# Seven-for-eight products taken one level further in v and p, with another test of the score bound and narrower reciprocals, in an attention and non-local kernel

## The chip, the cores and the metric

The kernel runs on one core of a Trainium2 chip, as one program. The metric is its device time in microseconds: the median of several runs. A core has TensorE (PE, with the weight loads shown apart as PEld), VectorE (DVE), ScalarE (ACT), GpSimd (POOL) and SyncE (SP, which here only issues DMAs). PE writes to PSUM alone: eight banks, each of 512 float32 numbers on 128 partitions. DVE and ACT read results out of there.

## What is computed

Two layers on x of shape (8, 512, 32, 32), all in float32. Layer 0 is attention with 8 heads over the 1024 positions of an image, layer 1 a non-local block with a normalization over the batch. Cut to what matters:

```python
q = conv1x1(x, Wq, bq); k = conv1x1(x, Wk, bk); v = conv1x1(x, Wv, bv)    # B, 8 heads, 64, 1024
attn = softmax(einsum('bhdn,bhdm->bhnm', q, k) * 64 ** -0.5, axis=-1)
x = x + conv1x1(einsum('bhnm,bhdm->bhdn', attn, v), Wp, bp)
g, theta, phi = conv1x1(x, g_w, g_b), conv1x1(x, theta_w, theta_b), conv1x1(x, phi_w, phi_b)
f = einsum('bcn,bdn->bcd', theta, phi) / 1024
z = conv1x1(einsum('bcd,bdn->bcn', f, g), W_w, W_b) + x
out = (z - mean(z)) * rsqrt(var(z) + 1e-5) * gamma + beta                   # over batch and positions
```

## The kernel before

**Stages.** The eight images go one after the other, and their stages are interleaved. In one turn b of the main loop: attention of image b; then q of image b+1, v of b+1, k of b+1; then the projection p of image b, theta and phi (tp), g with f in its midst (pg, pf), the product of f with W (pwf) and z. The last turns differ somewhat, and the last stage of all adds up z of the last images, takes the statistics and writes the outputs.

**Seven products.** A matrix product is cut into quadrants 11, 12, 21, 22, and seven products of sums of quadrants stand for the eight plain ones (the Winograd form of Strassen's method). `seven` (line 258) issues them. Sums of data quadrants, called t1 to t4, are DVE instructions into blocks of 128 x 1024 in a ring of ten (`ring`, tag e), which attention's exponentials use too. Sums of weights are made once and kept in DRAM (`keep`, `keep_inner`), from where each stage's weights are loaded again, two stages ahead.

**Products within products.** For q and k (and, for images 1 to 6, p) some of the seven are themselves replaced by seven smaller ones, the inner steps (`nested`, line 242). `INNER` says which: products 1, 2 and 6 for q and k, 1 and 2 for p, none for v. The inner steps need inner differences of their data quadrant, four DVE instructions of 128 x 256 each (`inner_sums`, `inner_parts`). Where three are replaced, the four left are issued in halves (`HALVES`), 16 units of PE work, and `STEPS` says how many inner steps follow each unit: none after units 0 to 2, one after 3 and 4, two after 5 to 12, one after 13 to 15. `READS` says after which units the finished quadrants are read out of PSUM. Where two are replaced there are 20 units and one step after each from unit 4 on.

**Banks.** PSUM is used as four pairs of banks (`bank`, tags s0 to s3). The inner steps have two pairs. The seven steps of an inner product go to three accumulators, in the order A B A B A C A, and each step's sum is read out by DVE (or ACT, where it is the first of its quadrant) before the accumulator is added to again. For every second inner product the two pairs change places, and its columns are the other half of each bank.

**Order.** The program is compiled by a scheduler that may move instructions, but those passed through `pe`, `dve` and `sp` stay in program order on their engine. All matmuls are. `fills` calls functions after given units of a stage, `between` after given products; in this way DVE work is placed by hand.

**The denominators.** Attention sums its exponentials over keys in `acc`; DMAs fold them into a tile `fold` with few partitions per head. `all_denominators` (line 526) lets PE add up the rest (`den`), takes the reciprocal on DVE as 128 x 512, where eight partitions hold the same row, writes 16 rows to DRAM, and `rows_of` reads them back, each row spread over 64 partitions, into `r`. `normalize` gives four DVE products of o by r, pinned. All of it lies in v of the next image: denominators after its product 1, the products after its product 5. t1 to t4 of o follow in k (line 901), and p needs them.

**The bound.** Exponentials are taken without subtracting the maximum. `bound_scores` (line 421) guards that: DVE takes the largest absolute value of q and k per channel (`peak_of`, line 396), PE adds their products per head (`heads`), DVE compares with `BOUND`, and POOL multiplies q by the outcome, 0 or 1. At the end the outcomes are counted, and if one is 0, a second, slower program (`shifted`) does the work anew.

Of the kernel before, what the change touches and what calls it, by code (L numbers as in the profile page):

```python
# [8 lines left out]
F32 = mybir.dt.float32  # L9
# [7 lines left out]
P = 128  # L17
HEADS = 8
EPS = 1e-5
BOUND = 60.0  # L20
# [10 lines left out]
def unshifted(ctx: ExitStack, tc: tile.TileContext, a: dict, out: bass.AP):  # L31
# [83 lines left out]
    INNER = {"WqT": (1, 2, 6), "WkT": (1, 2, 6), "WpT": (1, 2)}  # L115
# [26 lines left out]
    def weights(name, sums_done=False):  # L142

        n, w = loaded.pop(0)
        assert n == name
        if name not in kept:
            if not sums_done:
                weight_sums(w, corner[name])
            if name not in ("WqT", "WkT"):
                keep("plain" if name == "WpT" else name, w)  # L150
        return w
# [93 lines left out]
    def nested(name, stage, w, data, tags, first, add):  # L245

        slots = [bank(tag, f"{name}_in_{tag}") for tag in tags]
        goes_to = {1: ("11", "21", False), 6: ("12", "22", False), 2: ("21", "t4", True)}
        for n, (q, di, begins) in enumerate(goes_to[i] for i in INNER[stage]):
            a, d = inner_blocks(w, stage, n), data[f"inner {di}"]  # L250
            pair = slots[::-1] if n % 2 else slots
            begun = set()
            for _, wi, di, s, reads in SEVEN:
                ps = pair[s % 2 if s < 2 else 1][:, s // 2, n % 2 * 256:(n % 2 + 1) * 256]
                pe(nc.tensor.matmul(ps, a[wi], d[di], start=s not in begun, stop=True, skip_group_check=True))  # L255
                begun.add(s)
                for to, is_first in reads:
                    c = rows(q).start + int(to[0]) - 1
                    at = cols(q).start + (int(to[1]) - 1) * 256
                    (first if is_first and begins else add)((slice(c, c + 1), slice(at, at + 256)), ps)  # L260
                yield

    def seven(name, w, data, positions_out, first, add, between=None, early=False,
# [10 lines left out]
        if inner:  # L274
            free[:] = [tags[1], tags[2], tags[3], tags[0]]
            steps = nested(name, inner, w, data, tags[2:], first, add)
# [6 lines left out]
        for n, m in HALVES if three else ((n, None) for n in range(len(products))):  # L283
# [12 lines left out]
            work = [(*part, k) for part in (parts if m is None else parts[m:m + 1]) for k in range(nk)]  # L296
            if by_chunk and what in ("11", "s1t1"):
                work.sort(key=lambda one: one[4])
            for to_ps, at, lhsT, rhs, k in work:
                pe(nc.tensor.matmul(to_ps, lhsT(k), rhs(k), start=(s, at) not in begun, stop=(k == nk - 1),  # L300
                                    skip_group_check=True))
                begun.add((s, at))
                for ahead in (True, False):
                    for one, to, is_first in READS.get(unit, ()) if three and ahead == (unit < 15) else ():
                        read(((to, is_first),), slots[one])
                    for _ in range(next(counts, 0) if ahead else 0):
                        next(steps)
                if unit in fills:
                    fills[unit]()
                unit += 1  # L310
# [18 lines left out]
    heads = const.tile([P, P], F32, tag="heads", name="heads")  # L329
    nc.vector.memset(heads, 0.0)  # L330
# [13 lines left out]
    for i in range(WARM):  # L344
        pe(nc.tensor.matmul(ps[:, :P], heads, heads, start=True, stop=True))
# [18 lines left out]
    for j in range(2):  # L364
        nc.vector.memset(heads[j * D:(j + 1) * D, j * D:(j + 1) * D], 1.0)
    mv = const.tile([P, CC, 2], F32, tag="mv", name="mv")
    gates = const.tile([P, B * NPAIR], F32, tag="gates", name="gates")
# [9 lines left out]
    def heads_of(b, what, w, bias, data, pin=lambda ins: None, later=None, **how):  # L377

        t = mats.tile([P, CC, N], F32, tag=what, name=f"{what}_{b}")
        peak = small.tile([P, CC], F32, tag=f"peak_{what}", name=f"peak_{what}_{b}")  # L380

        def first(q, ps):
            if isinstance(q[0], slice):
                c = q[0].start
                nc.scalar.activation(t[:, c, q[1]], ps, AF.Identity, bias=bias[:, c:c + 1])
                return
            for m in range(2):
                c = rows(q).start + m
                if how.get("early") and q == "21":
                    nc.vector.tensor_scalar(t[:, c, cols(q)], ps[:, m, :], bias[:, c:c + 1], 1.0, ALU.add, ALU.mult)  # L390
                else:
                    nc.scalar.activation(t[:, c, cols(q)], ps[:, m, :], AF.Identity, bias=bias[:, c:c + 1])

        seven(f"p{what}_{b}", w, data, False, first, add_to(t, pin), **how)

        def peak_of(c):
            ins = nc.vector.tensor_reduce(peak[:, c:c + 1], t[:, c, :], AX.X, ALU.max, apply_absolute_value=True)
            if b == 0 or later is not None:
                dve(ins)

        for c in range(CC):
            if later is None:
                peak_of(c)
            else:
                later.append(lambda c=c: peak_of(c))
        return t, peak

    def values(b, w, data, between=None):
        v = mats.tile([P, NB, C], F32, tag="v", name=f"v_{b}")

        def at(q):
            return v[:, (int(q[1]) - 1) * NB // 2:int(q[1]) * NB // 2, (int(q[0]) - 1) * C // 2:int(q[0]) * C // 2]

        def as_v(ps):
            return ps.rearrange("p h (i f) -> p (h i) f", f=C // 2)

        seven(f"pv_{b}", w, data, True, lambda q, ps: nc.scalar.copy(at(q), as_v(ps)),  # L417
              lambda q, ps: dve(nc.vector.tensor_tensor(at(q), at(q), as_v(ps), ALU.add)), between)
        return v

    def bound_scores(b, q, k, peak_q, peak_k):

        nc.vector.tensor_tensor(peak_q, peak_q, peak_k, ALU.mult)
        ps = next_bank(f"bound_{b}")[:, 0, :]
        pe(nc.tensor.matmul(ps[:, :CC], heads, peak_q, start=True, stop=True))
        gate = gates[:, b * NPAIR:(b + 1) * NPAIR]
        nc.vector.tensor_scalar(gate, ps[:, :CC], BOUND / SCALE, 1.0, ALU.is_le, ALU.mult)  # L427
        for p in range(NPAIR):
            nc.gpsimd.tensor_scalar(q[:, p, :], q[:, p, :], gate[:, p:p + 1], 1.0, ALU.mult, ALU.mult)  # L429
# [6 lines left out]
    def attention(b, q, k, v, near_end, make_f=None):  # L436
# [89 lines left out]
        def all_denominators(ps):  # L526

            t = folded.pop("t")
            if b == 0:
                bias_product(t[:, 3, :], ps[:, 1, :CC])  # L530
            t, ps = t[:, 2, :], ps[:, 0, :]
            columns(ps, folds8, lambda j: t[:, j * 512:(j + 1) * 512])
            ri = t[:, :512]
            nc.vector.reciprocal(ri, ps)
            d = dram2.tile([16, 512], F32, tag="den", name=f"den_d_{b}")
            nc.sync.dma_start(d, ri.rearrange("(a s) n -> a s n", a=16)[:, 0, :])
            d = d.rearrange("(j g i) n -> g j (i n)", j=2, g=2)
            return d[0], d[1]

        def denominators(g, ps):  # L540
# [8 lines left out]
            d = dram2.tile([8, 512], F32, tag=f"den{g}", name=f"den_d_{b}_{g}")  # L549
            nc.sync.dma_start(d, ri.rearrange("(a s) n -> a s n", a=8)[:, 0, :])  # L550
            return d.rearrange("(j i) n -> j (i n)", j=2)
# [23 lines left out]
        for i in range(len(steps) + LAG):  # L575
# [8 lines left out]
            if b == 0 and i == 8:  # L584
                aside = join_bias(folded["t"][:, 3, :])
# [167 lines left out]
    late, z = {}, {}  # L753
# [90 lines left out]
    q, peak_q = heads_of(0, "q", weights("WqT", True), bq, data, early=True, by_chunk=True)  # L844
# [8 lines left out]
    k, peak_k = heads_of(0, "k", w, bk, data)  # L853
    keep_inner("WkT", w)
    load_w(nc.sync)
    v = values(0, weights("WvT"), data, {3: lambda: bound_scores(0, q, k, peak_q, peak_k)})
    load_w(nc.sync)
    held = {}
    for b in range(B):
# [23 lines left out]
        if not last:  # L883
            later, of_22, of_t4 = [], [], []
# [5 lines left out]
            q, peak_q = heads_of(b + 1, "q", weights("WqT"), bq, nxt["data"], dve, inner="WqT",  # L890
                                 later=later, fills=fills)
            load_w(nc.sync)

            def norm():
                nxt["products"] = normalize(denominators(next_bank(f"den_{b}")))

            v = values(b + 1, weights("WvT"), nxt["data"], {1: norm, 2: lambda: [one() for one in later], 5: lambda: nxt["products"]()})
# [7 lines left out]
            else:  # L905
                w_p = loaded[1][1]
                for unit, which in ((12, (3, 4)), (14, (5, 6))):
                    fills[unit] = lambda which=which: weight_sums(w_p, corner["WpT"], which, dve)
            later_k = []
            k, peak_k = heads_of(b + 1, "k", weights("WkT"), bk, nxt["data"], later=later_k, inner="WkT",  # L910
                                 fills=fills)
            if b:
                inner_sums(nxt["o"], "t4", dve)
            load_w(nc.sync)
# [22 lines left out]
        elif b > B - LATE and b != B - 2:  # L937
# [3 lines left out]
                       {5: lambda: b < B - 2 and of_theta.append(f_sums(b, tps[0], 0)), 1: lambda: [one() for one in later_k[:2]], 2: lambda: [one() for one in later_k[2:]],  # L941
                        4: lambda: bound_scores(b + 1, q, k, peak_q, peak_k)})
# [20 lines left out]

    last_z()


    good = const.tile([P, 1], F32, tag="good", name="good")
    nc.vector.tensor_reduce(good, gates, AX.X, ALU.min)
# [215 lines left out]
```

## Time and profile before

| | us |
|---|---|
| median of 3 runs | 2146.78 (2145.57 to 2147.17) |
| span of the profiled execution | 2143.6 |
| one turn of the loop, images 1 to 4 (606.52 to 869.50 in the chain of waits) | 262.98 |
| of it attention (606.46 to 716.48) | 110.0 |
| q, v, k, p, tp of image 2 | 22.91, 25.38, 22.80, 23.21, 24.40 |

In the profile, a line of groups gives busy time and the mean length of one instruction; matmuls overlap, so their pace is read from the starts of a row of them rather than from that mean. Each float32 matmul leaves two records. "idle before" is how long the engine stood before an instruction, and who released it. A stage's name is that of its PSUM tile: pq, pv, pk, pp, ptp, pg, pf, pwf, pz; those of inner steps end in in_s.

### The profile page before, as it was taken

To read this page: it belongs to the slowest core of one execution; us is meant where nothing else is said; L and a number is where in the kernel's file an instruction comes from. 1 tells how busy PE (TensorE), PEld (TensorE's weight loads), DVE (VectorE), ACT (ScalarE), POOL (GpSimd) and SP (SyncE) were. 2 spreads that over 40 slices of the span, in tenths; PEclk is the share of its full clock that TensorE was granted. 3 is DMA by queue.
4 is the path that set the end of the run, shared out by engine and by line. 5 is a ranking of instruction groups with operands and counts; after the bars stand their busy time and mean duration, and the time that the engine had idled before them with its cause. 6 is when DMAs were issued, how large, how long until landed. Compare 5 with 4: busy or idle time off the path is not lost.

```text
span 2143.6 us, 30444 instructions
## 1 busy us (share of the span) xinstructions
PE 2119.6 (99%) x12654; PEld 1123.3 (52%) x12654; DVE 1448.4 (68%) x1795; ACT 742.8 (35%) x848; POOL 193.2 (9%) x242
## 2 busy tenths in 40 slices
PE   9999999999999999999999999999999999999996
PEld 4534664356733567335673366633666347743462
DVE  6467667667676676766667667676675676756736
ACT  1464104641046310463105621066212652056106
POOL 0111000110001100011001100011000110011000
PEclk9999999999999999999999999999999999999998
DMA  6433443334143331433323342233434235122758
GB/s 242 137 46 58 136 166 127 49 71 129 73 131 49 79 116 73 133 50 83 109 102 109 48 100 99 97 107 50 108 132 161 42 45 139 52 60 39 227 197 341
DMA packets 53969, 231.05 MB, mean 108 GB/s; under 512 B 9792, under 2 KB 16192, under 8 KB 46272
## 3 DMA queue, kind: packets, MB, share of 16 engines
q1 hardware_dynamic: 42144, 199.26, 27.5%
q0 software_dynamic: 10192, 28.46, 11.0%
q8 instruction: 101, 1.65, 0.3%
q10 hardware_dynamic: 1488, 1.32, 0.2%
q14 instruction: 44, 0.36, 0.1%
HBM read 141.84 MB, written 46.27 MB: 88 GB/s over the span
## 4 chain that ended last, share of the span: by engine, by line
PE 96%; ACT 1%; DVE 1%; DMA 1%; issue 0%; SPq 0%; ACTq 0%; DVEq 0%
PE ps L462 21%; PE po L488 21%; PE pv L300 9%; PE ptp L300 9%; PE pp L300 7%; PE pk L300 6%; PE pq L300 5%; PE pg L300 4%; PE pk_in_s L255 3%; PE pq_in_s L255 3%; PE pz L300 2%; PE pf L658 2%; PE pp_in_s L255 2%; PE pwf L713 1%; ACT z L830 1%; PE pf L674 1%
## 5 line engine op out<-in xcount | busy, mean ns | idle before, releaser
L465 ACT ACTIVATE e<-ps 128x1024 f32<-128x1024 f32 x512 | 522.6, 1024 | 431.1 <-PE ps L462 425.6
L471 DVE TENSOR_TENSOR acc<-acc,e 128x1024 f32<-128x1024 f32 x384 | 470.0, 1224 | 143.7 <-ACT e L465 140.3
L462 PE MATMUL ps<-q,k 64*64 64x512 f32 x4096 | 529.4, 589 | 0.0
L488 PE MATMUL po<-e,v 64*64 64x512 f32 x4096 | 528.7, 589 | 0.0
L488 PEld LDWEIGHTS po<-e,v 64*64 64x64 f32 x4096 | 156.6, 133 | 282.9 <-issue 275.4
L462 PEld LDWEIGHTS ps<-q,k 64*64 64x64 f32 x4096 | 155.5, 133 | 283.8 <-issue 274.8
L501 POOL DMA_DIRECT2D fold<-acc x189 | 147.1, 779 | 978.9 <-DMA fold<-acc 576.6
L701 ACT ACTIVATE g<-pg,gb 128x512 f32<-128x512 f32 x31 | 21.3, 687 | 475.4 <-PE pg L300 475.3
L469 DVE TENSOR_TENSOR acc<-e,e 128x1024 f32<-128x1024 f32 x64 | 78.3, 1224 | 136.6 <-ACT e L465 136.6
L300 PE MATMUL pv<-w_WvT,t_x 128*128 128x256 f32 x512 | 116.4, 381 | 0.0
L300 PE MATMUL ptp<-w_tp,t_x 128*128 128x256 f32 x512 | 114.4, 379 | 0.0
L417 ACT COPY v<-pv 128x1024 f32<-128x1024 f32 x32 | 32.4, 1012 | 213.9 <-PE pv L300 213.9
L300 PEld LDWEIGHTS pv<-w_WvT,t_x 128*128 128x128 f32 x512 | 96.6, 190 | 18.5 <-issue 5.7
L300 PEld LDWEIGHTS ptp<-w_tp,t_x 128*128 128x128 f32 x512 | 97.3, 190 | 13.2
L300 PE MATMUL pq<-t_x,w_WqT 128*128 128x512 f32 x200 | 100.1, 592 | 0.8 <-DVE t_x L842 0.8
L300 PE MATMUL pp<-t_o,w_WpT 128*128 128x512 f32 x208 | 100.8, 592 | 0.0
L300 PE MATMUL pk<-t_x,w_WkT 128*128 128x512 f32 x200 | 100.0, 592 | 0.0
L429 POOL TENSOR_SCALAR q<-q,gates 128x1024 f32<-128x1024 f32 x32 | 35.1, 1109 | 718.4 <-DVE gates L427 718.4
L300 PE MATMUL ptp<-w_tp,x 128*128 128x256 f32 x384 | 87.4, 381 | 0.0
L300 PE MATMUL pv<-w_WvT,x 128*128 128x256 f32 x384 | 86.8, 379 | 0.0
L324 DVE TENSOR_TENSOR q<-q,pq_in_s 128x256 f32<-128x256 f32 x119 | 48.6, 420 | 51.1 <-PE pq_in_s L255 38.4
L324 DVE TENSOR_TENSOR k<-k,pk_in_s 128x256 f32<-128x256 f32 x119 | 47.9, 420 | 48.6 <-PE pk_in_s L255 36.0
(195 smaller groups left out, 2348.6 us busy)
## 6 DMA issues: line engine op xcount, KB each, us to landing
fold<-acc POOLq DMA_DIRECT2D x189, 128.0 KB, 3.1
w_WqT<-kept_WqT SPq DMA_DIRECT2D x7, 2368.0 KB, 8.8
w_WkT<-kept_WkT SPq DMA_DIRECT2D x7, 2368.0 KB, 8.8
r<-den_d SPq DMA_DIRECT2D x32, 512.0 KB, 6.9
x<-in_x_dram SPq DMA_DIRECT2D x30, 512.0 KB, 5.7
w_WpT<-kept_WpT SPq DMA_DIRECT2D x6, 2176.0 KB, 8.3
w_WvT<-kept_WvT SPq DMA_DIRECT2D x7, 1792.0 KB, 7.2
w_tp<-kept_tp SPq DMA_DIRECT2D x7, 1792.0 KB, 7.3
```

The lines of the kernel that those rows point to most:

```text
L255: pe(nc.tensor.matmul(ps, a[wi], d[di], start=s not in begun, stop=True, skip_group_check=True))
L300: pe(nc.tensor.matmul(to_ps, lhsT(k), rhs(k), start=(s, at) not in begun, stop=(k == nk - 1), skip_group_check=True))
L324: pin(nc.vector.tensor_tensor(at, at, ps if len(ps.shape) == 3 else ps.unsqueeze(1), ALU.add))
L417: seven(f"pv_{b}", w, data, True, lambda q, ps: nc.scalar.copy(at(q), as_v(ps)), lambda q, ps: dve(nc.vector.tensor_tensor(at(q), at(q), a ...
L429: nc.gpsimd.tensor_scalar(q[:, p, :], q[:, p, :], gate[:, p:p + 1], 1.0, ALU.mult, ALU.mult)
L462: pe(nc.tensor.matmul(ps[c * P // 2:(c + 1) * P // 2, j, :], k[r, p, keys], q[r, p, h * 512:(h + 1) * 512], start=True, stop=True, skip_gr ...
L465: nc.scalar.activation(e, ps, AF.Exp, scale=SCALE)
L469: nc.vector.tensor_tensor(accs[u], es[u, 0], e, ALU.add)
L471: ins = nc.vector.tensor_tensor(accs[u], accs[u], e, ALU.add)
L488: pe(nc.tensor.matmul(ps[j * D:(j + 1) * D, r, :], v[keys, m, (2 * p + j) * D:(2 * p + j + 1) * D], e[keys, j, :], start=(m == 0), stop=(m ...
L501: nc.gpsimd.dma_start(to, part_of, accum_op=ALU.add)
L658: pe(nc.tensor.matmul(to, theta[l][:, i, :], phi[r][:, i, :], start=(i == 0), stop=(i == NB // 2 - 1), skip_group_check=True))
```

## The change

There are four parts.

- v gets inner products: `INNER` has v with products 1, 2 and 6. In v, positions are on the partitions of the result, so an inner step is two matmuls with 128 columns each, and the two pairs of banks do not change places, which leaves one bank free. Into that bank the denominators are summed. The 32 matmuls of the four products left are taken two to a unit. The kept WvT holds its inner sums.
- p gets a third inner product, 6, which needs the inner differences of quadrant 22 of o; they are made after k, behind those of t4. p is now issued in halves, with `STEPS` and `READS` of three.
- The bound is tested on the denominators. `heads`, `peak_of`, `bound_scores`, the gates and POOL's products are gone. All denominators are kept in `dens` (128 x 512), and at the end DVE tests that each lies between 1e-20 and 1e20.
- The reciprocals are taken on 128 x 64: ACT copies the sums out of PSUM, a DMA writes 16 rows to DRAM, a DMA reads them back as 128 rows of 64, DVE takes the reciprocal into `dens`, a DMA writes that to DRAM, and from there r is read as before. Sums are issued after unit 3 of v, the reciprocal and r after unit 8, the products of o by r after unit 15, the last one.

The sums of k and its reads are now pinned with `dve`. The last image's denominators, whose reciprocal stays 128 x 512, are read into `dens` by two DMAs ahead of the last stage. The small product for the bias of p (image 0 alone), which was taken beside its denominators, stands ahead of v.

```diff
-BOUND = 60.0
+SANE = 1e20
...
-    INNER = {"WqT": (1, 2, 6), "WkT": (1, 2, 6), "WpT": (1, 2)}
+    INNER = {"WqT": (1, 2, 6), "WkT": (1, 2, 6), "WvT": (1, 2, 6), "WpT": (1, 2, 6)}
...
-    def nested(name, stage, w, data, tags, first, add):
+    def nested(name, stage, w, data, tags, first, add, positions_out=False):
         slots = [bank(tag, f"{name}_in_{tag}") for tag in tags]
+        if positions_out:
+            rest["bank"] = slots[0][:, 1, :]
...
-            pair = slots[::-1] if n % 2 else slots
+            pair = slots[::-1] if n % 2 and not positions_out else slots
...
-                pe(nc.tensor.matmul(ps, a[wi], d[di], start=s not in begun, stop=True, skip_group_check=True))
+                if positions_out:
+                    ps = ps.rearrange("p (i f) -> p i f", f=P)
+                    for i in range(2):
+                        pe(nc.tensor.matmul(ps[:, i, :], d[di][:, i * P:(i + 1) * P], a[wi], start=s not in begun and not i,
+                                            stop=True, skip_group_check=True))
+                else:
+                    pe(nc.tensor.matmul(ps, a[wi], d[di], start=s not in begun, stop=True, skip_group_check=True))
...
-            work = [(*part, k) for part in (parts if m is None else parts[m:m + 1]) for k in range(nk)]
+            each = len(parts) // 2
+            work = [(*part, k) for part in (parts if m is None else parts[m * each:(m + 1) * each]) for k in range(nk)]
...
+                if three and positions_out and not i % 2:
+                    continue
...
-    def bound_scores(b, q, k, peak_q, peak_k):
-
-        nc.vector.tensor_tensor(peak_q, peak_q, peak_k, ALU.mult)
-        ps = next_bank(f"bound_{b}")[:, 0, :]
-        pe(nc.tensor.matmul(ps[:, :CC], heads, peak_q, start=True, stop=True))
-        gate = gates[:, b * NPAIR:(b + 1) * NPAIR]
-        nc.vector.tensor_scalar(gate, ps[:, :CC], BOUND / SCALE, 1.0, ALU.is_le, ALU.mult)
-        for p in range(NPAIR):
-            nc.gpsimd.tensor_scalar(q[:, p, :], q[:, p, :], gate[:, p:p + 1], 1.0, ALU.mult, ALU.mult)
...
             columns(ps, folds8, lambda j: t[:, j * 512:(j + 1) * 512])
-            ri = t[:, :512]
-            nc.vector.reciprocal(ri, ps)
-            d = dram2.tile([16, 512], F32, tag="den", name=f"den_d_{b}")
-            nc.sync.dma_start(d, ri.rearrange("(a s) n -> a s n", a=16)[:, 0, :])
-            d = d.rearrange("(j g i) n -> g j (i n)", j=2, g=2)
-            return d[0], d[1]
+            den = t[:, :512]
+            nc.scalar.copy(den, ps)
+            d = [dram2.tile([16, 512], F32, tag=f"den{i}", name=f"den{i}_d_{b}") for i in range(2)]
+            nc.sync.dma_start(d[0], den.rearrange("(a s) n -> a s n", a=16)[:, 0, :])
+            many, one = (of.rearrange("a (x n) -> (a x) n", x=8) for of in d)
+            wide = t[:, 512:576]
+            nc.sync.dma_start(wide, many)
+
+            def rest():
+                to = dens[:, b * 64:(b + 1) * 64]
+                dve(nc.vector.reciprocal(to, wide))
+                nc.sync.dma_start(one, to)
+                rows = d[1].rearrange("(j g i) n -> g j (i n)", j=2, g=2)
+                return rows[0], rows[1]
+
+            return rest
...
-            v = values(b + 1, weights("WvT"), nxt["data"], {1: norm, 2: lambda: [one() for one in later], 5: lambda: nxt["products"]()})
+            v = values(b + 1, weights("WvT"), nxt["data"], inner="WvT",
+                       fills={3: sums, 8: norm, 15: lambda: nxt["products"]()})
...
-            k, peak_k = heads_of(b + 1, "k", weights("WkT"), bk, nxt["data"], later=later_k, inner="WkT",
-                                 fills=fills)
+            k = heads_of(b + 1, "k", weights("WkT"), bk, nxt["data"], dve, inner="WkT", fills=fills)
             if b:
                 inner_sums(nxt["o"], "t4", dve)
+                inner_sums(nxt["o"], "22", dve)
...
+    for to, d in own:
+        nc.sync.dma_start(to, d)
     last_z()
 
-    good = const.tile([P, 1], F32, tag="good", name="good")
-    nc.vector.tensor_reduce(good, gates, AX.X, ALU.min)
+    good, sane = const.tile([P, 1], F32, tag="good", name="good"), block("sane")[:, 0, :]
+    nc.vector.tensor_scalar(sane, dens, 1.0 / SANE, 1.0, ALU.is_ge, ALU.mult)
+    nc.vector.scalar_tensor_tensor(sane, dens, SANE, sane, ALU.is_le, ALU.mult)
+    nc.vector.tensor_reduce(good, sane, AX.X, ALU.min)
```

## The prediction

> **What bounds the kernel now.** I read the page first (busy times, then the chain of waits), then one image by windows, then the timelines of PE and VectorE (DVE) where stages meet.
>
> ```profile
> span 2143.6 us, 30444 instructions
> PE 2119.6 (99%) x12654; PEld 1123.3 (52%) x12654; DVE 1448.4 (68%) x1795; ACT 742.8 (35%) x848; POOL 193.2 (9%) x242
> PE 96%; ACT 1%; DVE 1%; DMA 1%; issue 0%; SPq 0%; ACTq 0%; DVEq 0%
> ```
>
> PE is the bound and its chain has next to no waits. So a change gains only what it takes out of PE's own stream, and every wait it puts there is paid in full. Three stages of image 2, by windows (v, k, p):
>
> ```profile
> 739.39:764.77 25.38, 25.38 (x117) 21.39 (x116) 16.09 (x13) 3.04 (x3) 0.00 (x0) 1.00 0.64 181
> 764.77:787.57 22.80, 22.80 (x75) 14.05 (x74) 15.54 (x28) 6.66 (x11) 0.00 (x0) 1.00 0.27 99
> 787.57:810.78 23.21, 23.21 (x69) 12.92 (x68) 16.36 (x30) 0.00 (x0) 0.00 (x0) 1.00 0.22 79
> ```
>
> After the length comes PE's busy time, which fills each stage; the third sum is DVE's, some 16 of 23 us. DVE has room on average; the question is when. PE's pace comes from chain pieces (start, length, what, records; a float32 matmul leaves two records):
>
> ```profile
> 580.95 6.25 PE pf L658 x56
> 764.94 3.43 PE pk L300 x8
> 810.95 17.27 PE ptp L300 x80
> 828.21 0.12 PE bound L425 x2
> 828.33 7.01 PE ptp L300 x32
> ```
>
> A record of 128 columns takes 6.25/56 = 0.1116 us, of 256 columns 0.2159, of 512 columns 0.429. Now DVE at the seams, from its timeline (start, length):
>
> ```profile
> 763.79 3.49 DVE L571 TENSOR_TENSOR o<-o,r 128x1024 f32<-128x1024 f32 x3
> 769.13 0.42 DVE L324 TENSOR_TENSOR k<-k,pk_in_s 128x256 f32<-128x256 f32 x1 [1.84 <-ACT k L392]
> ...
> 787.77 0.42 DVE L324 TENSOR_TENSOR k<-k,pk_in_s 128x256 f32<-128x256 f32 x1
> 788.11 2.35 DVE L324 TENSOR_TENSOR k<-k,pk 128x1024 f32<-128x1024 f32 x2
> 790.37 0.42 DVE L218 TENSOR_TENSOR i_t_o<-t_o 128x256 f32<-128x256 f32 x1
> ...
> 791.84 1.40 DVE L602 SCALAR_TENSOR_TENSOR x<-pp,bp,x 128x512 f32<-128x512 f32 x2
> 793.16 0.41 DVE L324 TENSOR_TENSOR x<-x,pp_in_s 128x256 f32<-128x256 f32 x1
> ```
>
> k begins at 764.77; the last product of o by r ends at 767.28, 2.5 us into k, before DVE has anything of k to read. p begins at 787.57, and there DVE is busy without a gap (two last sums of k, four i_t_o, two quadrants of x) until it takes up p's first inner result, 5.6 us in. That margin is the thing to watch.
>
> **What the Trainium skill says.** "PSUM — Partial Sum Buffer", section "PSUM bank collisions raise a hardware error": guard PSUM by bank, not by address. The trace agrees. In q the ninth inner matmul writes another half of a bank than the seventh, and its weight load still waits for the seventh's read (DVE 726.94 + 0.42, then this on PEld):
>
> ```profile
> 727.41 0.19 PEld L255 LDWEIGHTS pq_in_s<-i_t_x,w_WqT 128*128 128x128 f32 x1 [0.30 <-DVE q L324]
> ```
>
> The same page, "Engine vs sequencer instructions": VectorE's and ScalarE's queues are strict FIFO; here DVE's order above is that of the program. "DMA: Bandwidth & Descriptors", "Two DMAs through the same engine are not ordered": a DMA that reads what another wrote must wait for its landing; here SP issued r 1.84 us after den_d (750.91 to 752.75).
>
> **Gains on PE.** (1) v, 7 images: three products of 8 matmuls of 256 columns (48 records x 0.2159 = 10.36) become 42 inner steps' matmuls, 21 steps of two of 128 columns (84 x 0.1116 = 9.37): 0.99 each, 6.9 in all. (2) p, 6 images: one more product of 4 matmuls of 512 (8 x 0.429 = 3.43) becomes 14 records of 256 (3.02): 0.41 each, 2.5. (3) The bound: tp takes 24.40 us (810.78 to 835.18), its 112 records 24.18: 0.22 each, x 8 = 1.8. Sum 11.2 us. Nothing else is on PE: the peaks (64 x 1.2 us, DVE), 28 of the 32 us of long reciprocals (3.36 each, 7 of them: 23.5), POOL's 35 us of gating were all hidden behind PE, and cost nothing before.
>
> **Waits on PE.** A release costs: PE's last result to DVE's start 0.20 (787.57 to 787.77), an add of 256 columns 0.42, DVE's end to the weight load 0.05 (727.36 to 727.41), load to matmul 0.10 (an estimate: half of the 0.19 load row, as loads overlap).
>
> (a) Inside v. An inner product's seven steps use banks A B A B A C A. In q and k the pair is turned for the second product, so its first step goes to B; with positions_out it isn't turned, so step 8 goes to A at once after step 7 (both in unit 7, with no other matmul between). It waits 0.20 + 0.42 + 0.05 + 0.10 = 0.77. Steps 14 and 15 have a unit's 0.86 us between them, enough. 0.77 x 7 = 5.4. Bounds: 0 if halves of a bank were kept apart, 0.9 if DVE is late. I take 0.77.
>
> (b) Start of k. The products of o by r move from after product 5 of v to unit 15, the last, behind v's own last sums. v becomes 25.38 - 0.99 + 0.77 = 25.16 us. From k's start DVE has: last inner read 0.20, two sums of 1024 columns 0.54 and 1.67 (pitch 1.13, as at 788.11 to 790.37), four products 2.80, 3.93, 5.07, 6.20 (pitch 1.14), and k's first inner read at 7.33 to 7.75. The third inner step of k adds to the bank which that read empties: it can start at 7.90, and would have at 770.79 - 764.77 = 6.02. PE loses 1.88, x 7 = 13.2. Behind this read stand k's second read and t_o; they don't add, since each next step has 0.86 to 1.7 us. It holds if r has landed. That chain, from v's start: den after unit 3 ends near 5.1; ACT's copy 0.58 (COPY o<-po row) 5.8; a DMA to memory at 1.84, but the load of w_WkT (2368 KB, 8.8 us, issued at 0.2) runs until 9.0, so 7.7 to 10.9; a DMA back, nearest row again 1.84: 9.6 to 12.8; reciprocal of 64 columns, estimate 3.36/8 = 0.42, 12 to 13.5; DMA out, 14 to 15.5; four r issues in 2.4 us, the last at 15.8 to 17.3, each landing 6.7 us after its issue (median; 11.5 at most): by 24, at worst 29. Products 3 and 4 need the last two at 25.16 + 5.07 = 30.2, so at least 1 us is spare. SP's waits there hold only the load of w_WpT behind them, due a stage later.
>
> (c) Start of p. The third inner product needs inner differences of quadrant 22 of o, four more DVE instructions pinned after k. From p's start: 2.80 after k's sums as above; eight differences x 0.367 (four took 1.47) to 5.74; two quadrants of x at 0.66 to 7.06; first inner read to 7.47; third step at 7.62. With seven steps in three products the inner steps also begin a unit earlier and come in pairs, so the third is due at 6.02 (as in k), where before it was due at 794.44 - 787.57 = 6.87 and the read was done at 6.00. PE loses 1.60, x 6 = 9.6. Bounds: 0 if the compiler, which may move p's own unpinned reads, puts them ahead of the four differences.
>
> (d) Later in p, quadrants are first written by DVE (0.66 twice), where in k ACT does it; in units 9 to 12 that leaves the inner reads 0.3 and 0.4 us late by the same counting. I take half: 0.34 x 6 = 2.0, bounds 0 and 4.
>
> (e) Ends. Twelve small sums for the kept WvT (0.29 each, 3.5 us of DVE) and four for WpT fall beside attention and stages where PE has work; cost 0, or 1 if that cover were gone. The test at the end has three DVE instructions on 512 columns (near 0.4, 0.74, 0.6) instead of a tiny one, and two small DMAs on SP ahead of the last stage; DVE has gaps of 0.3 to 0.8 there. 0 to 1.8, I take 0.4. Loading w_WvT with its inner blocks (2368 instead of 1792 KB) is issued a stage of attention ahead, 0. New ACT copies in v (4 of 0.47, 0.58 for den) fall on an engine busy for 3 of 25 us: 0. The bias product of image 0 only moves: 0.
>
> Sum: -11.2 + 5.4 + 13.2 + 9.6 + 2.0 + 0.4 = +19.4 us on the profiled span: 2163.0. The median of the runs stands 3.2 above the span (2146.8 against 2143.6), so 2166.2.
>
> **Rivals.** (R1) p doesn't stall, the adds being put first: without the 9.6 of (c) it is 2156.6. For: p's reads are unpinned. Against: i_t_o stands before them today. (R2) Not slower: DVE reaches k's first read by 5.45 us after k's start, so that (b) is nothing, and the same at p: 2146.8 - 11.2 + 5.4 = 2141.0. Its place is those two reads; it decides once they are done 2 us sooner than I count. For: DVE loses over 100 us of other work. Against: that work lay elsewhere, and the order here is pinned. (R3) r lands late: two more DMA trips stand in its chain. Each microsecond past 30.2 is a microsecond of k; 3 us late gives 3 x 7 = 21 more, 2187. For: r took up to 11.5 us to land. Against: nothing else is loaded then.
>
> **How the numbers follow.** Forecast 0.60, R1 0.18, R2 0.12, R3 0.10. The range reaches from below R1 up to half of R3: 2149 to 2178; R2 and the far half of R3, 0.17, stay out. 0.2%, about what a measurement here can tell from no change, is 4.3 us. Faster comes from R2 alone, 0.12; the same is the ground between R2 and R1, 0.06; slower the rest, 0.82.
>
> **What would show it.** v near 25.2 us with one gap of 0.8 after step 7; k near 24.7 with one gap of 1.9 before its third inner step, released by DVE, with o<-o,r just ahead; p near 24.4, released by DVE x; tp 24.2. If k stays at 22.8, (b) is wrong and with it the sign; if v shows no gap, (a) is; if DVE's products wait for r, it is R3.

## Result and profile after

The changed kernel takes 2179.03 us (median of 4 runs, 2178.30 to 2179.52), the kernel before 2146.18 us (4 runs, 2145.41 to 2147.17): 1.0153 times as long, 95% interval 1.0141 to 1.0166. The profiled span grew by 33.1 us. The direction was forecast, the size was not: 19.4 us were expected.

The page of the changed kernel, with its span, the busy times and the shares of the chain of waits:

```profile
span 2176.7 us, 31163 instructions
PE 2120.1 (97%) x12926; PEld 1129.0 (52%) x12926; DVE 1428.9 (66%) x1916; ACT 750.2 (34%) x876; POOL 158.2 (7%) x210
PE 90%; DVE 6%; ACT 1%; DMA 1%; issue 1%; ACTq 0%; DVEq 0%; SPq 0%
```

PE's busy time is about what it was (2120.1 against 2119.6), although its stream is some 11 us shorter when it runs freely: PE's modelled ends take part of a wait for work (v of image 2 counts 24.73 us of PE below, and takes 24.40 us in all where nothing waits, in experiment 6). DVE has less to do than before, and yet its share of the chain went from 1% to 6%. The four stages of image 2, by windows (v, k, p, tp; after the length the busy time and records of PE, weight loads, DVE, ACT and POOL):

```profile
747.41:773.77 26.36, 24.73 (x154) 21.89 (x153) 11.11 (x21) 5.11 (x8) 0.00 (x0) 1.00 0.62 177
773.77:798.53 24.76, 23.13 (x76) 13.89 (x75) 20.00 (x32) 5.64 (x10) 0.00 (x0) 1.00 0.26 99
798.53:823.69 25.16, 23.60 (x76) 13.80 (x75) 19.45 (x41) 0.00 (x0) 0.00 (x0) 1.00 0.20 73
823.69:848.22 24.53, 24.41 (x114) 21.20 (x113) 16.20 (x17) 0.00 (x0) 0.00 (x0) 1.00 0.11 38
```

Each stage was full of PE before. Now v, k and p each hold some 1.6 us without PE. Lengths against before: v +0.98, k +1.96, p +1.95, tp +0.13. Over the images that have each form, 0.98 x 7 + 1.96 x 7 + 1.95 x 6 + 0.13 x 6 = 33.1, less 0.2 at each of the two other places where the bound's product is gone. So these four stages hold nearly all of the loss. (Image 1, ahead of whose v the bias product now stands, has its share elsewhere: 0.81 ahead of v, 0.00 in v, 2.25 in k.) Where in them the time goes, the chain of waits tells (start, length, what). Where the chain leaves PE for ACT or DVE, that work released PE's next instruction:

```profile
751.06 1.02 ACT v L422
...
752.11 0.43 DVE v L423
...
752.59 1.08 PE pv_in_s L429 x4
...
759.55 0.46 PE pv_in_s L260 x4
...
760.03 0.43 DVE v L423
...
760.50 0.71 PE pv_in_s L260 x4
...
779.09 0.87 PE pk L312 x2
...
779.97 1.22 DVE o L575
781.19 0.34 DVE k L338
...
781.58 1.13 PE pk_in_s L263 x4
...
804.00 1.00 DVE i_o L218 x3
805.00 0.66 DVE x L607
805.66 0.34 DVE x L338
...
806.04 1.13 PE pp_in_s L263 x4
...
813.90 0.74 DVE x L607
814.65 0.34 DVE x L338
...
815.03 1.13 PE pp_in_s L263 x4
```

Read from the top: in v a wait ahead of `den` (line 429) that was not forecast; a wait of DVE's 0.43 us after the seventh inner step, forecast as (a); the start of k behind a product of o by r (line 575), forecast as (b); the start of p behind the differences of o (`i_o`, line 218), (c); and one of two later waits in p, (d).

The wait ahead of `den` is the new thing. The timeline of the changed kernel there, with the idle time of an engine and its releaser in brackets:

```profile
751.06 1.01 ACT L422 COPY v<-pv 128x1024 f32<-128x1024 f32 x1 [8.64 <-PE pv L312]
752.11 0.42 DVE L423 TENSOR_TENSOR v<-v,pv_in_s 128x256 f32<-128x256 f32 x1 [1.81 <-ACT v L422]
752.58 0.20 PEld L429 LDWEIGHTS pv_in_s<-fold,folds 128*64 128x64 f32 x4 [1.30 <-DVE v L423]
```

`den` writes the second bank of the pair `pv_in_s`. The first inner step has just written the first bank. That step's sum is an addition to quadrant 11, which ACT must first copy out of PSUM (1.01 us), so DVE reads it late, and the weight load of `den` waits for that read, though `den` touches another bank.

DVE at the two seams, from its timeline:

```profile
776.57 4.62 DVE L575 TENSOR_TENSOR o<-o,r 128x1024 f32<-128x1024 f32 x4
781.11 0.74 DVE L338 TENSOR_TENSOR k<-k,pk_in_s 128x256 f32<-128x256 f32 x2
...
799.19 2.35 DVE L338 TENSOR_TENSOR k<-k,pk 128x1024 f32<-128x1024 f32 x2
...
802.92 0.42 DVE L218 TENSOR_TENSOR i_o<-o 128x256 f32<-128x256 f32 x1
803.25 0.74 DVE L607 SCALAR_TENSOR_TENSOR x<-pp,bp,x 128x512 f32<-128x512 f32 x1
...
805.58 0.74 DVE L338 TENSOR_TENSOR x<-x,pp_in_s 128x256 f32<-128x256 f32 x2
```

The four products run without a gap, so r was there: rival R3 did not happen. At p the scheduler did put one of p's own reads (803.25) among the differences of o, but the inner read still comes after all of them, as (c) counted; R1 did not happen either.

### The profile page after: what moved, and what is told of

It reads as the page before. It is cut to its first block, busy times and chain, and to the rows that moved or that the text cites. A ratio compares the mean times of both kernels' runs of the same rounds, so it can differ in the third digit from the quotient of the medians.

```text
span 2176.7 us, 31163 instructions
## 1 busy us (share of the span) xinstructions
PE 2120.1 (97%) x12926; PEld 1129.0 (52%) x12926; DVE 1428.9 (66%) x1916; ACT 750.2 (34%) x876; POOL 158.2 (7%) x210
## 4 chain that ended last, share of the span: by engine, by line
PE 90%; DVE 6%; ACT 1%; DMA 1%; issue 1%; ACTq 0%; DVEq 0%; SPq 0%
PE ps L457 20%; PE po L483 20%; PE ptp L312 9%; PE pv L312 6%; PE pq L312 5%; PE pk L312 4%; PE pg L312 4%; PE pp L312 4%; PE pv_in_s L260 3%; PE pq_in_s L263 3%; PE pz L312 2%; PE pk_in_s L263 2%; PE pp_in_s L263 2%; DVE k L338 2%; PE pf L663 2%; PE pwf L718 1%
## 5 line engine op out<-in xcount | busy, mean ns | idle before, releaser
L423 DVE TENSOR_TENSOR v<-v,pv_in_s 128x256 f32<-128x256 f32 x119 | 49.5, 421 | 106.8 <-PE pv_in_s L260 90.9
L312 PE MATMUL pv<-w_WvT,t_x 128*128 128x256 f32 x400 | 101.5, 381 | 0.0
L312 PEld LDWEIGHTS ptp<-w_tp,x 128*128 128x128 f32 x384 | 73.0, 190 | 10.8 <-issue 1.0
L312 PEld LDWEIGHTS pv<-w_WvT,t_x 128*128 128x128 f32 x400 | 69.5, 191 | 11.6 <-issue 5.7
L403 ACT ACTIVATE k<-pk,bk 128x512 f32<-128x512 f32 x50 | 31.6, 683 | 97.7 <-PE pk L312 97.7
```

## Experiments

Seven kernels start from the changed kernel, the last from the kernel before. Single runs are compared by their spans with the changed kernel's 2176.7 us, and stage by stage on image 2.

**1. Turn the pair for v's second product too.** This undoes the adjacency behind (a) alone.

```diff
-            pair = slots[::-1] if n % 2 and not positions_out else slots
+            pair = slots[::-1] if n % 2 else slots
```

> The changed kernel with one edit: in v the two pairs of banks change places for the second inner product, as they do in q and k. Theory (the eighth inner step waits because it goes to the accumulator that the seventh has just filled): the gap of 0.78 us after step 7 of v is gone in all seven images, v 26.36 to 25.6, total 5.5 us less than 2179.0, so 2173.5. Rival (DVE is simply behind in v, and the wait only moves): v or k keeps the 0.78, total within 1 us of 2179.0.

Span 2170.9, 5.8 less; v 25.58, that is -0.78, the other three stages as they were. The chain of this kernel, ahead of `den` and at the seventh and eighth inner step:

```profile
749.34 1.02 ACT v L422
...
759.58 0.89 PE pv_in_s L260 x8
```

The seventh and eighth steps now run as one piece, and the wait ahead of `den`, behind ACT's copy, stays. (a) is right, in place and in size.

**2. `den` one unit earlier,** before the first inner step has written anything, into the same bank.

```diff
+            if positions_out:
+                rest["pairs"] = [bank(tag, f"{name}_in_{tag}") for tag in tags[2:]]
+                rest["bank"] = rest["pairs"][0][:, 1, :]
...
-                       fills={3: sums, 8: norm, 15: lambda: nxt["products"]()})
+                       fills={2: sums, 8: norm, 15: lambda: nxt["products"]()})
```

> The changed kernel with the sums of denominators issued after unit 2 of v, before the first inner step, in the same free bank. Theory (den waits because it shares its pair of banks with the first inner step, whose read on DVE waits for ACT's copy of quadrant 11): nothing of the pair is unread then, the gap of 1.37 us ahead of den is gone, v 26.36 to 25.0, total 9.6 us less, 2169.4. Rival A (den waits for the folded tile to land): the gap stays or grows, since den is asked for 1.3 us sooner. Rival B (the wait passes to the first inner step, which must then wait for ACT's copy of den): half or more of the 1.37 stays, ahead of that step.

v 25.18, -1.18. The chain of this kernel:

```profile
745.19 2.59 PE pv L313 x12
747.78 1.01 PE pv_in_s L430 x4
748.79 1.06 PE pv L313 x4
```

No wait before or after `den`. So the read of the first inner step was what held it. The gap was 1.28 us: the inner step's four records, from 750.86, are through by 751.31 at their pace of 0.1116, and `den` starts at 752.59. A switch of 0.09 stays where nothing waits (754.74 to 754.83 in experiment 5, by the same working), hence about 1.18 x 7 = 8.3 us rather than 9. The span fell by 7.3 only (2169.4): in image 5, PE waits 1.3 us once ahead of `den`, with no releaser shown (see the end of the next section).

**3. Two of the products of o by r at the end of v, two inside k.**

```diff
-                       fills={3: sums, 8: norm, 15: lambda: nxt["products"]()})
+                       fills={3: sums, 8: norm, 15: lambda: nxt["products"](((0, 0), (0, 1)))})
...
+            fills[6] = lambda: nxt["products"](((1, 1),))
+            fills[8] = lambda: nxt["products"](((1, 0),))
```

> The changed kernel with two of the four products of o by r moved from after unit 15 of v to units 6 and 8 of k. Theory (k's third inner step waits for the first inner read, which stands behind four products on DVE): DVE reaches that read 2.27 us sooner, the gap of 1.9 us is gone, k 24.77 to 22.8, total 13.8 us less, 2165.2. Rival (DVE has no room in k, 15.5 of 22.8 us without them): the two products come back as waits later in k, k stays above 24.

Span 2163.4, 13.3 less; k 22.87, that is -1.89, the rest unchanged. Its chain runs through the place of the wait:

```profile
775.18 0.86 PE pk L312 x2
776.04 0.86 PE pk_in_s L263 x4
```

(b) is right: the same DVE work, placed a few units later, costs next to nothing (k stays 0.07 above the kernel before).

**4. Two inner products in p, as before the change.** Product 6 of p is computed plainly again, and the four differences of o for it are left out.

```diff
-    INNER = {"WqT": (1, 2, 6), "WkT": (1, 2, 6), "WvT": (1, 2, 6), "WpT": (1, 2, 6)}
+    INNER = {"WqT": (1, 2, 6), "WkT": (1, 2, 6), "WvT": (1, 2, 6), "WpT": (1, 2)}
...
-                inner_sums(nxt["o"], "22", dve)
```

> The changed kernel with two inner products in p, as before the change, and without the four differences of quadrant 22 of o. Theory (waits for DVE at p's start and at its units 10 and 12, and for t_x at the start of tp, come from the third inner product): p 25.15 to 23.21, tp 24.53 to 24.18, total 13.7 us less, 2165.3. Rival (p's DVE work is late because k was): p keeps 1 us or more above 23.21.

Span 2163.3, 13.4 less. p and tp of this kernel, by windows:

```profile
796.39:819.60 23.21, 23.21 (x69) 12.95 (x68) 16.52 (x31) 0.00 (x0) 0.00 (x0) 1.00 0.21 80
819.60:843.78 24.18, 24.18 (x114) 21.32 (x113) 14.99 (x15) 0.00 (x0) 0.00 (x0) 1.00 0.11 39
```

p falls by 1.95, and tp by 0.35 with it. The second was not in the prediction: with three inner products DVE is behind at the end of p as well, and makes the first sum of x for tp (t_x) late. The timeline of the changed kernel, DVE at tp's start:

```profile
826.06 1.22 DVE L206 TENSOR_TENSOR t_x<-x 128x1024 f32<-128x1024 f32 x1
```

It ends at 827.28; tp began at 823.69, and its second product, due 3.5 us later, needs this sum. In the chain PE stands still for 0.10 us there and then takes 20.96 us for 96 records, where 96 x 0.2159 are 20.73.

**5. `den` after unit 3 still, but in another pair of banks.** Is the wait kept for the pair of banks as one tile, or does something else hold `den`? The new pair is the one that the next unit of v writes; `den` gets the bank that this unit does not write.

```diff
+            if positions_out:
+                slots[1] = bank(tags[1], f"{name}_1")
+                rest["bank"] = slots[1][:, 1, :]
```

> The changed kernel with the sums of denominators still after unit 3 of v, but in the idle second bank of the pair that the four large products use from unit 4 on. Theory 1 (waits are kept per bank, and den waited for some other reason than the first inner step's bank): a gap of 1.3 us ahead of den stays, total 2179. Theory 2 (waits are kept per pair of banks, the tile): den starts at once, and unit 4, which writes the first bank of that pair, waits for ACT's copy of den, which stands behind ACT's copy of quadrant 11: den ends near 5.0 us into v, the copy 0.8 us later, so unit 4 loses about 0.8 us, v 25.8, total 2175. Theory 3 (per bank, and den's wait came from sharing the very bank): no gap at all, v 25.0, total 2170.

The timeline of this kernel:

```profile
754.83 1.08 PE L430 MATMUL pv<-fold,folds 128*64 128x512 f32 x4
755.54 0.42 DVE L424 TENSOR_TENSOR v<-v,pv_in_s 128x256 f32<-128x256 f32 x1 [1.81 <-ACT v L423]
755.96 0.59 ACT L528 COPY fold<-pv 128x512 f32<-128x512 f32 x1 [0.45 <-PE pv L430]
...
756.60 1.13 PE L313 MATMUL pv<-w_WvT,t_x 128*128 128x256 f32 x4 [0.69 <-ACT fold L528]
```

`den` follows the inner step at once, 0.7 us before DVE begins to read that step's sum (755.54). So it was the pair that held it, and neither the landing of `fold` nor anything else. And the next unit of v, which writes the other bank of the new pair, now waits 0.69 us until ACT has copied `den` out. The wait moved with the pair: theory 2. v takes 25.93, 0.43 less than in the changed kernel. "PSUM — Partial Sum Buffer" of the Trainium skill, section "PSUM bank collisions raise a hardware error", which the prediction drew on, asks to guard by bank; in this kernel the waits come by whole pair. The function `bank` makes each pair one tile of 128 x 2 x 512, so the unit of the waits is that of the program's tiles. That tiles of one bank each would free `den` is likely from this, but was not tried. The total (2179.61) says little here, since the very first stage, which the edit does not touch, took 29.8 us instead of 25.4 in this run. Without these 4.4 us the span (2177.9) is 3.2 below that of the changed kernel, and 0.43 x 7 are 3.0.

**6. The four edits together.**

> The changed kernel with the four edits together: pairs turned in v, sums of denominators after unit 2, two products of o by r in k, two inner products in p. Theory (the waits were the whole loss, and add): v 24.4, k 22.87, p 23.21, tp 24.17; against before 0.98 x 7 less in v, 0.23 x 8 less in tp, 0.07 x 7 more in k: 8.2 us less than before, ratio 0.9962. Rival (a wait hides behind another, and comes out once that is gone): above 2146 us, no gain.

2139.01 us (median of 6 runs, 2138.74 to 2139.76), against 2145.99 of the kernel before (10 runs): 0.9968 times, 95% interval 0.9956 to 0.998. By this 0.3% it is faster than the kernel before, too. Its windows for the four stages, and the shares of its chain:

```profile
737.35:761.75 24.40, 24.40 (x154) 21.66 (x153) 11.06 (x21) 5.11 (x8) 0.00 (x0) 1.00 0.69 191
761.75:784.61 22.86, 22.86 (x76) 13.97 (x75) 19.94 (x32) 5.66 (x10) 0.00 (x0) 1.00 0.26 99
784.61:807.82 23.21, 23.21 (x69) 12.92 (x68) 16.52 (x31) 0.00 (x0) 0.00 (x0) 1.00 0.22 80
807.82:831.99 24.17, 24.17 (x113) 21.28 (x112) 14.98 (x15) 0.00 (x0) 0.00 (x0) 1.00 0.11 39
```

```profile
PE 97%; DVE 1%; ACT 1%; issue 0%; DVEq 0%; ACTq 0%
```

PE fills each stage again. v is 0.98 shorter than before the change, tp 0.23: these are the gains (1) and (3) as forecast, with nothing lost against them. The four edits add up: alone they took 5.8, 7.3, 13.3 and 13.4 us from the span, 39.8 in all (the last of them gives up gain (2)), and together 39.8 (2176.7 to 2136.9). So no wait was hidden behind another. Of the 8.2 us expected against the kernel before, 7.0 came; image 5 again has the one wait of 1.3 us ahead of `den`, and its v takes 25.78.

**7. Can p keep its third inner product?** Experiment 6 with three inner products in p, the four differences of o spread over units 4 to 7 of p instead of pinned ahead of it.

```diff
-                inner_sums(nxt["o"], "22", dve)
+                of_p = inner_parts(nxt["o"], "22", dve)
...
+                dict(zip((4, 5, 6, 7), of_p)) if 0 < b < B - 1 else ())
```

> As e6_all_four, but with three inner products in p, the four differences of quadrant 22 of o moved from the start of p to its units 4 to 7. Theory (the four differences make the wait at p's start, and DVE's first writes of quadrants those in units 10 and 12 and at the start of tp): the first gap falls from 1.6 to 0.2 us, the later 0.75 and the 0.36 of tp stay, p 23.7, tp 24.5, 5 us more than e6_all_four. Rival (all of p's waits came from the late start): p 22.8, tp 24.2, 2.5 us less than e6_all_four.

2143.94 us, 4.9 more than experiment 6. p takes 23.82 and tp 24.53. The chain of this kernel holds DVE nowhere in the first 11 us of p; the later wait stays:

```profile
799.39 0.74 DVE x L607
800.13 0.34 DVE x L339
...
800.51 1.13 PE pp_in_s L261 x4
```

DVE writes the quadrant of x (0.74 us), and only then adds the inner result to it. These later waits and tp's 0.36 together are more than the 0.41 that the third product saves. So not with this placing: spreading the differences takes the wait at p's start down to 0.27 us, but not those behind DVE's first writes of quadrants.

**8. The bound by itself: the kernel before without it.** Left out are the peaks, their product with `heads` and the multiplication of q by the outcome; the gates are set to 1.

```diff
-        for c in range(CC):
-            if later is None:
-                peak_of(c)
-            else:
-                later.append(lambda c=c: peak_of(c))
...
+    nc.vector.memset(gates, 1.0)
```

> The kernel before, leaving out the bound on scores: no peaks on DVE (64 instructions), no product with heads on PE, no products of q by gates on POOL; the gates are set to 1 once. Theory (all but the small product on PE was hidden): tp 24.40 to 24.17, total 1.8 us less than before. Rival (75 us of DVE and 35 of POOL were partly on the path): 5 us less or more.

2144.08 us against 2145.99, and tp 24.17 instead of 24.40, no other stage of image 2 changed. So the 64 peaks on DVE and POOL's multiplications had indeed cost nothing, and the gain (3) is PE's own 0.22 per image.

## Why the prediction was right in direction and short in size

**Gains.** (1) -0.98 in v, forecast 0.99; (3) -0.23 in tp, forecast 0.22 (experiments 6 and 8). (2), 0.41 in p, was not seen by itself; it stands in the sums below.

**(a)** forecast 0.77, measured 0.78. **(b)** forecast 1.88, measured 1.96 in the window of k, of which experiment 3 takes back 1.89. The chain has PE idle from 779.96 to 781.58, and the four records after it take 1.13 instead of 0.86: 1.62 + 0.27 = 1.89. The counting of DVE's queue from k's start was right to 0.1 us. **(c)** forecast 1.60, measured 1.60 (PE is idle for 1.34 us, the 0.27 come on top).

**(d)** was counted as 0.3 and 0.4 and then halved to 0.34. It came as 0.38 twice, 0.76 (before the records at 815.03 and at 818.85). The halving had no reason from the profile; the missing 0.41 x 6 is 2.5 us. (The "p near 24.4" among the signs had left (d) out; the sum of the terms gave 24.7, and 25.16 was measured.)

**The step that failed** is the one on `den`. The prediction said "den after unit 3 ends near 5.1" as a plain link of the chain of r: the only question it asked of `den` was when r would land. It took for granted that PE reaches `den` without a wait. Read by bank, as it read PSUM, there was nothing to wait for, as `den` has a bank to itself; but the row that it showed for this (727.41, in q) has both matmuls in one bank, and so in one pair, and fits either unit. What the runs show: `den` waits 1.28 us for the read of the other bank of its pair, because that read waits for ACT's copy, and ends 6.3 us into v (753.66). The wait moves with the pair (experiment 5) and goes when `den` stands ahead of the first inner step (experiment 2). 1.18 x 7 = 8.3 us.

**tp** was to gain 0.22 and no more was asked of it. With p's third inner product it is 0.35 longer than without, x 6 = 2.1 us (experiment 4): that DVE would end p late was put at nothing. And k lost 0.08 more than counted, x 7 = 0.6 us.

19.4 + 8.3 + 2.5 + 2.1 + 0.6 = 32.9, of 33.1 measured. **(e)** had 0.4 us for the end and 0 for the small sums. From the last image's tp to the end it took 104.96 us against 105.16 before, so the 0.4 did not show; what is left, 0.2, leaves no room for more. The narrow reciprocal took 0.55 us (estimated 0.42), on a DVE that was idle there. **R2,** the side of no loss, failed as its own condition says: DVE reached k's first inner read 7.3 us after k's start, not by 5.45. But experiment 6 shows that it is a matter of place: with two products moved, the order on DVE leaves PE no wait. What spoke for R2, that DVE loses over 100 us of work, left out the work that the change adds: DVE's busy time fell by 19.5 us only (1448.4 to 1428.9). And "28 of the 32 us" of long reciprocals does not fit the 23.5 beside it, which is the measured sum; no term rests on it.

**Image 5** alone has the wait of 1.3 us ahead of `den` in experiments 2 and 6. The timeline of experiment 6 there:

```profile
1260.19 0.86 POOL L497 DMA_DIRECT2D fold<-fold  x1 [6.80 <-DMA fold<-fold]
...
1265.08 1.08 PE L430 MATMUL pv_in_s<-fold,folds 128*64 128x512 f32 x4 [1.31 <-issue]
```

This last DMA into `fold` lands 4.8 us after its issue, at 1264.99, and the weight load of `den` starts 0.06 us later; it is the same 0.06 in experiment 2. In the other images `fold` has landed 1.1 to 2.7 us before that load. So here rival A of experiment 2 holds, in one image of seven: `den` is asked for before its data is there. The DMA is late because POOL, which issues it, stood still for 5.52 us ahead of an earlier one (at 1252.62), against 2.64 in image 2. These 2.9 us more, where image 2 has 1.6 to spare, make the wait of 1.3.

**Open.** What POOL waited for there is not shown by the trace.

## What to carry to other kernels

When PE fills its stages and its chain has no waits, count the DVE work between the last result of one stage and the first accumulator that the next stage needs back; work placed at the end of a stage belongs to the start of the next. Where something is put into a free half of a buffer, find out from the trace for which unit waits are kept (a bank, a pair, a tile), and ask what the other half is waiting for. Where counting gives a delay, carry the whole of it into the sum, unless a row of the profile shows that part of it is hidden.

## What the runs showed of the hardware

A small DMA behind a big one on SP's queue. `den_d` (16 rows) is written soon after the load of w_WkT (2368 KB) has been issued, and the DMA that reads it back is issued only once `den_d` has landed. The timeline of SP in experiment 2, image 2:

```profile
745.22 0.33 SPq L134 DMA_DIRECT2D w_WkT<-kept_WkT  x1
749.45 0.51 SPq L530 DMA_DIRECT2D den_d<-fold  x1
753.85 0.34 SPq L533 DMA_DIRECT2D fold<-den_d  x1
```

The read-back comes 4.4 us after `den_d`, and 0.2 us after the load's landing (8.4 us after 745.22). In the changed kernel `den_d` is issued 6.7 us after the load rather than 4.2, and its read-back 1.94 us later (754.32 to 756.26), again 0.3 us after the load's landing. In the changed kernel and in experiments 2 and 6 this holds for images 2 to 7: the read-back is issued 0.2 to 0.3 us after the load has landed, also in image 5, where the load takes 11.3 to 11.7 us. Once the load has landed, the DMAs that wait for the next small one (`den_d` again, from `dens`) are issued 1.45 us after it (757.38 to 758.83 in experiment 2). So the small one lands with the big one ahead of it, as the upper end of the prediction's chain of r had assumed; that chain had the time for it. Whether it is held by the queue that both use, or by what they share beyond it, was not tried.
